# A four-part graph network on one core: three hops joined into one stream, and attention layers whose rows are prepared by finished node tiles

## The chip, the cores and the metric

The kernel runs on one core of one Trainium2 chip. The metric is device time in microseconds (us) of one execution; the time before is the median of three runs. Engines are named as the profile names them: PE (matrix products; PEld is its weight load), DVE (VectorE), ACT (ScalarE), POOL (GpSimd) and SP, whose queue issues most DMA transfers.

## The reference

A graph of 3125 nodes with 128 features each has 103125 edges (50000 in both directions and one loop per node), sorted by target. Four residual parts follow each other; every part takes the layer norm and relu of x and adds its result to x.

```python
h = jnp.maximum(_layernorm(x), 0.0)
x = x + hops(h)        # 3 hops:
    # left = agg[head] @ q_w;  right = tanh(rel * agg[tail] @ k_w)
    # w = softmax over the edges of a head of sum(left * right)
    # agg = segment_sum(w * rel * agg[tail], head) / max(count, 1)
    # agg = agg / max(norm(agg), 1e-12);  out = out + agg + h
h = jnp.maximum(_layernorm(x), 0.0)
x = x + gat(h)         # 3 layers, 4 heads of 32 features:
    # e = leaky_relu(alpha_s[src] + alpha_d[dst]);  softmax over the edges of a target
    # out = segment_sum(xs[src] * alpha, dst) + bias;  relu between layers
h = jnp.maximum(_layernorm(x), 0.0)
x = x + gcn(h)         # 2 graph convolutions with degree norms, then two dense layers
h = jnp.maximum(_layernorm(x), 0.0)
x = x + relation(h)    # one attention over the edges of a target with rel_emb, then tanh(. @ neigh_w)
```

## The kernel before, in words

**Tiling.** Nodes lie in T = 28 tiles of Q = 112 rows. First (to about 1010 us) the edges are counted and sorted into cells: one cell per pair of a target tile and a source tile, with up to 128 edges on the partitions. What does not fit its cell goes to OV = 3 overflow cells per column. A *column* is one node tile as the side that is summed over; it has NG = 8 *groups*, seven of K = 4 cells and one of the three overflow cells. Node tiles are also taken by *quads*, four at a time, seven quads in all (`quads()`).

**Gathering by matrix products.** Rows of nodes are held three times in bfloat16 (`parts`, split by `in_parts`, L738 to L741, two ACT copies and two DVE subtractions per quad), and one-hot matrices (`oh`, `own`) multiply them. Overflow rows come from a table in HBM with indirect DMAs of POOL's queue (`gather`, L703): `rows_d` for the hops, `gat_d` for the layers.

**Hops and the relation attention.** `attend` (L776) is called once per hop and once at the end. It is a software pipeline written out by hand: the list `order` holds pairs of a stage and a lag, and each step `i` runs the stage for group `i - lag`, so that the engines' queues hold instructions in just that order (`in_order`). The stages are: `s_load` (lag 0: one-hot loads, overflow gathers), `s_hot`, `s_rel`, `s_rows` (L828 on PE), `s_comb` (L836 DVE, times the relation), `s_turn` (L844 PE transposes, L846 ACT copy), `s_right` (L852 PE, L854 ACT Tanh), `s_score` (L860 PE, L862 DVE), `s_most` to `s_less` (maximum per node, L874 to L906 DVE), `s_exp` (L910 ACT Exp), and `s_sum` (lag 21, L918 PE), which at a column's end copies sum and denominator out of PSUM (L921, L922). 224 groups and 21 lags make 245 steps. In hop 0 further work rides along: relation rows, masks and degrees are made and kept in HBM for the later hops.

After each hop a tail for all tiles follows (L1074 to L1101): `over_in` once in hop 0 (its load is L684), r = 1 / denominator / count, agg times r, Square and reduce, Sqrt (L1090), agg times the reciprocal norm (L1094), the add to `xs` on POOL (L1096), `in_parts`, the store to `rows_d` (L1100) and `sides` (transposes L747, product with q_w L762, copy L763).

**The three layers.** The order here is a scheduler's: the program's order with priorities, under waits for data and for tile buffers of the pools `rows1` and `sums1`. `norm_relu` runs first. `layer_rows` (L1117 to L1148) per quad transposes h, multiplies by the layer's weights (L1135), copies (xw), splits into `parts` and stores `gat_d`; then it stores the alphas of all targets (L1145) and spreads them over 112 partitions as `arow` (L1148, four broadcasts). `layer_sums` (L1150) then goes through the columns. Each column is prepared: `c_load` (overflow gathers, `absent` load L1168), `c_rows` (one-hots L1179), in layer 0 also `c_hot` and seven `c_cells` (L1198 to L1236, counts and masks of the column, kept for the later layers), `c_most` (L1248, the greatest alpha of the present edges per head, two halves on DVE), `c_node`, `c_weights` (Exp at L1288). Its groups run `g_load` (eq), `g_rows` (L1305 PE), `g_weigh` (L1313 DVE, rows times the head's weight; L1316 ACT copy of the weights) and `g_sum` (L1325 PE), the last of a column followed by L1329 to L1336 (division, bias, relu). The add of the layers' result to `xs` comes after the third layer (L1372).

**GCN and end.** In the pool `work2` follow the degree norm n_src, the layer norm, the product with n_src (L1430), two `sum_rows`, the dense layers, and the layer norm for the relation attention; after that a tail (L1500 to L1513) divides, transposes, multiplies by nw, takes Tanh, adds to `xs`, and writes the output in two DMAs.

Of the kernel before, what the change touches and what calls it, by code (L numbers as in the profile page):

```python
# [16 lines left out]
P = 128  # L17
D = 128
# [424 lines left out]
def by_cells(ctx: ExitStack, tc: tile.TileContext, edges, x, E, edge_emb, q_w, k_w, Ws, Wd, att_s, att_d,  # L443
# [25 lines left out]
    rows_d = tc.dram_tile([NP, D], F32, name="rows_d")  # L469
    gat_d = tc.dram_tile([NP, D + H], F32, name="gat_d")  # L470
# [69 lines left out]
    kindD = node.tile([P, T, COL], I32, name="kindD")  # L540
    outO = node.tile([P, T, OV], I32, name="outO")
    inO = node.tile([P, T, OV], I32, name="inO")
    posO = node.tile([P, T, OV], I32, name="posO")
    movO = node.tile([P, T, OV, 4], F32, name="movO")
# [14 lines left out]
    def lay_out(rows, tab, pp, pname):  # L559
# [3 lines left out]
        nonlocal ownS, kindS  # L563
        edge = hop_.enter_context(tc.tile_pool(name="edge", bufs=1))
        ownS = edge.tile([P, T, COL], BF16, name="ownS")
        kindS = edge.tile([P, T, COL], I32, name="kindS")
        with tc.tile_pool(name="lay", bufs=1) as lp:
# [114 lines left out]
    def over_in():  # L682
        lay = work.tile([P, T, OV, 4], F32, name="layD", bufs=1)
        nc.sync.dma_start(lay, slots_o[:T * NO, :].rearrange("(s p k) f -> p s k f", p=P, k=OV))  # L684
        nc.vector.tensor_copy(overO[:, 0], lay[:, :, :, 0])
        nc.vector.tensor_sub(overO[:, 1], lay[:, :, :, 3], lay[:, :, :, 0])
        nc.vector.tensor_copy(kindD[:, :, T:], lay[:, :, :, 2])
        nc.vector.tensor_copy(inO, lay[:, :, :, 3])
        f = work.tile([P, T * OV], F32, name="fD", bufs=1)
        nc.vector.tensor_copy(f, lay[:, :, :, 1].rearrange("p s k -> p (s k)"))  # L690
        pt = pm.tile([P, K, P], F32, name="pm")
        nc.tensor.transpose(pt[:T * OV, 0, :], f, ident)
        rb = work.tile([T * OV, P], BF16, name="rbD", bufs=1)
        nc.scalar.copy(rb, pt[:T * OV, 0, :])
        nc.sync.dma_start(bass.AP(tensor=dst_own.tensor, offset=dst_own.offset + T * P,
                                  ap=[[COL * P, T], [P, OV], [1, P]]), rb)
# [68 lines left out]
    def row_tile(table, c, t0, n, p=Q, name="row", bufs=3):  # L765

        t = work.tile([p, HALF * P], BF16, name=name, bufs=bufs)
# [8 lines left out]
    def attend(oh_d, table, idx, side, den, sums, combine, rel_d, masks, rel_rows=None, right=None, aside=None,  # L776
               column_end=None):


        cols = {}  # L780
        groups = [(c, g) for c in range(T) for g in range(NG)]
        st = {}
        H1 = NG // 2
# [5 lines left out]
        def s_load(c, g):  # L789
# [6 lines left out]
            if g == 0:  # L796
                over_rows[c] = work.tile([P, OV, D], F32, name="orow", bufs=2)
                for k in range(OV):
                    gather(over_rows[c][:, k, :], table, idx[:, c, k:k + 1])
            if rel_rows:  # L800
                rel_rows[0](s, c, g)
            if aside:
                aside(c * NG + g)

        def s_hot(c, g):
# [4 lines left out]
            if rel_rows:  # L810
                rel_rows[1](st[c, g], c, g)

        def s_rel(c, g):
            s, m = st[c, g], width(g)
            if not rel_rows:
# [3 lines left out]
        def s_rows(c, g):  # L819
# [10 lines left out]
            if rel_rows:  # L830
                rel_rows[2](s, c, g)

        def s_comb(c, g):
            s, m = st[c, g], width(g)
            s["v"] = vs[(c * NG + g) % len(vs)]
            nc.vector.tensor_tensor(s["v"][:, :m, :D], s["rows"][:, :m, :], s["rel"][:, :m, :], combine)  # L836
            if rel_rows:
# [46 lines left out]
        def s_diag(c, g):  # L884
# [7 lines left out]
            if column_end:  # L892
# [19 lines left out]
        def s_sum(c, g):  # L912
# [7 lines left out]
            if g == NG - 1:  # L920
                nc.scalar.copy(sums[:, c, :], acc[:Q, :D])  # L921
                nc.scalar.copy(den[:, c:c + 1], acc[:Q, D:D + 1])  # L922
            del st[c, g]

        def mask(i):
# [4 lines left out]
        order = [(s_sum, 14 + w), (s_exp, 13 + w), (s_less, 12 + w), (s_spread_most, 11), (s_turn_most, 10), (s_most, 9),  # L930
                 (s_comb, 5), (s_score, 8), (s_diag, 10), (s_right, 7), (s_turn, 6), (mask(2), 7), (mask(1), 6),
                 (mask(0), 5), (s_rows, 4), (s_hot, 2), (s_rel, 3), (s_load, 0)]
        with in_order(tc):
            for i in range(len(groups) + order[0][1]):
                for f, d in order:
                    if 0 <= i - d < len(groups):
                        f(*groups[i - d])
# [6 lines left out]
    den = hops.tile([Q, T], F32, name="den")  # L944
# [3 lines left out]
    bank = work = ownS = kindS = None  # L948
# [24 lines left out]
    with tc.tile_pool(name="work0", bufs=3) as work:  # L973
# [95 lines left out]
        for hop in range(3):  # L1069
            attend(src_oh, rows_d, outO, side, den, agg, OP.mult, src_rel, (other_load, other_make, other_keep),  # L1070
                   None if hop else (rel_load, rel_hot, rel_make, rel_keep), kw,
                   rel_ahead if hop else over_by_target, None if hop else degree)
            kept_out()
            if hop == 0:  # L1074
                over_in()
                nc.vector.tensor_scalar_max(cnt, deg_src, 1.0)
                nc.vector.reciprocal(cnt, cnt)
            r = work.tile([Q, T], F32, name="r", bufs=1)
            nc.vector.tensor_scalar_max(r, den, 1e-30)
            nc.vector.reciprocal(r, r)  # L1080
            nc.vector.tensor_mul(r, r, cnt)
            nr = work.tile([Q, T], F32, name="nr", bufs=1)
            for n0, n1 in quads():
                m = n1 - n0
                nc.vector.tensor_mul(agg[:, n0:n1, :], agg[:, n0:n1, :],
                                     r[:, n0:n1].unsqueeze(2).to_broadcast([Q, m, D]))
                sq = work.tile([Q, K, D + H], F32, name="res", bufs=2)
                nc.scalar.activation(sq[:, :m, :D], agg[:, n0:n1, :], AF.Square)
                nc.vector.tensor_reduce(nr[:, n0:n1], sq[:, :m, :D], AX.X, OP.add)
            nc.scalar.activation(nr, nr, AF.Sqrt)  # L1090
            nc.vector.tensor_scalar_max(nr, nr, 1e-12)
            nc.vector.reciprocal(nr, nr)
            for n0, n1 in quads():
                nc.vector.tensor_mul(agg[:, n0:n1, :], agg[:, n0:n1, :],  # L1094
                                     nr[:, n0:n1].unsqueeze(2).to_broadcast([Q, n1 - n0, D]))
                nc.gpsimd.tensor_add(xs[:, n0:n1, :], xs[:, n0:n1, :], agg[:, n0:n1, :])  # L1096
                if hop < 2:
                    in_parts(agg, n0, n1)
            if hop < 2:
                nc.sync.dma_start(node_rows(rows_d), agg)  # L1100
                sides(agg, side, qw)  # L1101

    hop_.close()

    with tc.tile_pool(name="work1", bufs=1) as work1:
        h = big.tile([Q, T, D], F32, name="agg")
# [4 lines left out]
        brow = work1.tile([P, D], F32, name="brow")  # L1111
# [3 lines left out]
        def layer_rows(l):  # L1115

            af = work.tile([Q, H, T], F32, name="af", bufs=1)  # L1117
            wx = work.tile([P, W4 + H], F32, name="wx", bufs=1)
            for w_, a_, to in ((Ws, att_s, D), (Wd, att_d, W4)):
                w = work.tile([P, H, C], F32, name="wl", bufs=2)  # L1120
                nc.scalar.dma_start(w.rearrange("p h c -> p (h c)"), w_[l])
                a = work.tile([P, H, C], F32, name="al", bufs=2)
# [5 lines left out]
                nc.vector.tensor_reduce(wx[:, to:to + H], a, AX.X, OP.add)  # L1128
            nc.scalar.dma_start(brow, bass.AP(tensor=gat_b.tensor, offset=gat_b.offset + l * D, ap=[[0, P], [1, D]]))
            for n0, n1 in quads():  # L1130
                hT = transposed(h, n0, n1)
                xw = work.tile([Q, K, W4 + H], F32, name="xw", bufs=3)
                for n in range(n0, n1):
                    pw = pm.tile([P, 512], F32, name="pm")
                    nc.tensor.matmul(pw[:Q, :W4 + H], hT[:, n - n0, :], wx, start=True, stop=True)  # L1135
# [1082 lines left out]
```

## Time and profile before

| | us |
|---|---|
| median of 3 runs | 7420.47 (7419.32 to 7425.95) |
| the profiled execution | 7405.67, its span 7403.9 |
| counting, sorting, laying out | 0 to about 1030 |
| three hops and their tails | to about 3793 |
| three layers | to 6243 |
| GCN, dense layers | to about 6700 |
| relation attention, tail | to 7403.9 |
| column, hop 0 / hops 1 and 2 / relation | 34.2 / 29.5 / 22.9 |
| column, layer 0 / layers 1 and 2 | 34.9 / 21.3 |
| busy share: PE, DVE, ACT, POOL | 83%, 76%, 42%, 49% |

A column's time is the distance between the ends of two neighbouring columns, which is read from the instruction that closes each (L921 and L1331). Between the last column of a stage and the first of the next lies a *seam*. A row of a window reads: the window, its length, then for PE, PEld, DVE, ACT and POOL the busy us and the number of instructions, the granted clock of PE as a share, the busy share of the DMA engines, and GB/s. A group's row reads: line, engine, operation, output and inputs, shapes, count, busy us and mean ns, idle time before it with what ended it.

### The profile page before, as it was taken

How to read it: one execution, taken by the hardware profiler on the slowest of the kernel's cores; microseconds unless marked ns; L12 is line 12 of the kernel's file. 1: busy time of each engine (PE TensorE's matmuls, PEld its weight loads, DVE VectorE, ACT ScalarE, POOL GpSimd, SP SyncE). 2: the span in 40 equal slices, each digit the busy share in tenths (PEclk: the TensorE clock that was granted, in tenths of full speed). 3: DMA queues.
4: the chain of work that ended last, by engine and by line, in shares of the span. 5: the costliest groups of instructions: out<-in, count | busy, mean ns of one | idle time of the engine just before them, and what ended most of it. 6: DMA issues, size and time to landing. Idle time of an engine off the chain costs nothing. (4 is left out here: it accounts for less than half of the span.)

```text
span 7403.9 us, 157726 instructions
## 1 busy us (share of the span) xinstructions
PE 6157.7 (83%) x59400; PEld 5175.9 (70%) x59400; DVE 5642.0 (76%) x12038; ACT 3098.9 (42%) x8419; POOL 3645.8 (49%) x3360
## 2 busy tenths in 40 slices
PE   5877729999989998999957878857775776988998
PEld 3443328888878887888846777747775776767998
DVE  8887628888866666666658999969997998237887
ACT  3766514444444444444437777720001001114554
POOL 2777767665468885777833433314431332341110
PEclk9887759999999999999977898878886888999999
DMA  2100025554467775777747888757766775556665
GB/s 64 25 19 17 12 54 156 151 148 145 135 175 208 204 208 146 213 208 203 205 116 231 242 246 255 239 163 211 205 192 175 207 204 163 144 151 183 213 213 155
DMA packets 686935, 1222.52 MB, mean 165 GB/s; under 512 B 129398, under 2 KB 450056, under 8 KB 684820
## 3 DMA queue, kind: packets, MB, share of 16 engines
q1 hardware_dynamic: 567060, 996.40, 45.5%
q0 software_dynamic: 109120, 208.86, 11.3%
q8 instruction: 473, 7.75, 0.5%
q10 hardware_dynamic: 9984, 7.07, 0.3%
q14 instruction: 298, 2.44, 0.1%
HBM read 915.61 MB, written 296.27 MB: 164 GB/s over the span
## 5 line engine op out<-in xcount | busy, mean ns | idle before, releaser
L1248 DVE CUSTOM_DVE_ANT_0 junk<-arow,absent 112x1568 bf16<-112x1568 f32 x672 | 1203.6, 1791 | 58.6 <-DMA absent<-absent_d 54.7
L1325 PE MATMUL pa<-v,eq 128*112 128x132 f32 x5208 | 831.1, 308 | 333.9 <-ACT v L1316 236.9
L703 POOL DMA_INDIRECT ahead<-in_L_gnn_rel_emb_dram,kindD x868 | 961.1, 1107 | 265.7 <-issue 254.7
L862 DVE SCALAR_TENSOR_TENSOR z<-other,pm 128x448 f32<-128x448 bf16 (+1 forms) x896 | 541.8, 605 | 617.2 <-PE pm L860 429.0
L1325 PEld LDWEIGHTS pa<-v,eq 128*112 128x112 f32 x5208 | 709.9, 198 | 372.1 <-ACT v L1316 247.8
L918 PE MATMUL pa<-v,z 128*112 128x129 f32 x6944 | 949.1, 279 | 4.6 <-ACT z L910 4.6
L854 ACT ACTIVATE right<-pm 128x512 f32<-128x512 f32 (+1 forms) x672 | 392.7, 584 | 1297.5 <-PE pm L852 1295.5
L703 POOL DMA_INDIRECT orow<-gat_d,inO x252 | 465.2, 1846 | 927.4 <-DVE ndp L1264 600.4
L918 PEld LDWEIGHTS pa<-v,z 128*112 128x112 f32 x6944 | 817.4, 177 | 20.3 <-ACT z L910 5.8
L373 POOL DMA_INDIRECT slots<-pay,pos x610 | 669.7, 1098 | 266.0 <-issue 182.2
L860 PE MATMUL pm<-side,right 128*128 128x112 f32 x5208 | 686.3, 274 | 4.3 <-DVE z L862 3.3
L844 PEld LDWEIGHTS pm<-ident,v 128*128 128x128 f32 x3472 | 431.3, 143 | 363.0 <-issue 274.6
L852 PE MATMUL pm<-vT,kw 128*128 128x512 f32 (+1 forms) x1344 | 684.2, 591 | 0.8 <-DVE z L862 0.8
L828 PE MATMUL pg<-parts,oh 112*128 112x128 bf16 x9408 | 663.9, 220 | 22.4 <-DMA oh<-src_oh 15.3
L1305 PE MATMUL pg<-parts,oh 112*128 112x128 bf16 x7056 | 557.7, 233 | 106.3 <-DMA oh<-oh_d 35.0
L860 PEld LDWEIGHTS pm<-side,right 128*128 128x128 f32 x5208 | 634.9, 192 | 6.1 <-issue 3.4
L846 ACT COPY vT<-pm 128x512 f32<-128x512 f32 (+1 forms) x896 | 511.3, 571 | 293.7 <-PE pm L844 221.7
L828 PEld LDWEIGHTS <-oh 112*128 112x128 bf16 x9408 | 600.2, 98 | 33.3 <-issue 24.2
L836 DVE TENSOR_TENSOR v<-pg,rel 128x512 f32<-128x512 f32 x700 | 479.7, 685 | 170.5 <-PE pg L828 111.6
L703 POOL DMA_INDIRECT orow<-rows_d,inO x252 | 241.1, 957 | 745.0 <-DVE v L836 484.1
L1305 PEld LDWEIGHTS <-oh 112*128 112x128 bf16 x7056 | 502.4, 106 | 111.4 <-issue 97.2
L844 PE MATMUL pm<-ident,v 128*128 128x128 f32 x3472 | 528.6, 274 | 22.5 <-DVE v L836 22.3
(372 smaller groups left out, 12645.9 us busy)
## 6 DMA issues: line engine op xcount, KB each, us to landing
eq<-eq_d SPq DMA_DIRECT2D x784, 224.0 KB
rel<-src_rel SPq DMA_DIRECT2D x392, 256.0 KB
dst_rel<-ahead POOLq DMA_DIRECT2D x196, 256.0 KB
rel<-dst_rel SPq DMA_DIRECT2D x196, 256.0 KB
other<-other_d SPq DMA_DIRECT2D x392, 112.0 KB
eq_d<-eqf SPq DMA_DIRECT2D x196, 224.0 KB
absent<-absent_d SPq DMA_DIRECT2D x56, 686.0 KB
ct<-count_d SPq DMA_DIRECT2D x56, 686.0 KB
```

What stands on the lines that cost most here:

```text
L373: st = nc.gpsimd.indirect_dma_start(out=slots, out_offset=bass.IndirectOffsetOnAxis(ap=pos[:m, k:k + 1], axis=0), in_=pay[:m, k0 + k, :], ...
L703: return nc.gpsimd.indirect_dma_start(out=to, out_offset=None, in_=table, in_offset=bass.IndirectOffsetOnAxis(ap=index, axis=0))
L828: nc.tensor.matmul(pg[:, k, :], h["oh"][:, (e0 + k) * P:(e0 + k + 1) * P], parts[:, g * K + k, i, :D], start=(i == 0), stop=(i == 2))
L844: nc.tensor.transpose(pT[:, k, :], s["v"][:, k, :D], ident)
L846: nc.scalar.copy(s["vT"][:, :m, :], pT[:, :m, :])
L852: nc.tensor.matmul(pK[:, :m, :], right, s["vT"][:, :m, :], start=True, stop=True)
L860: nc.tensor.matmul(pS[:, k, :], s["vT"][:, k, :], side[:, c, :], start=True, stop=True)
L862: nc.vector.scalar_tensor_tensor(s["z"], s.pop("other")[:, :m, :], MASK, pS[:, :m, :], op0=OP.mult, op1=OP.add)
L918: nc.tensor.matmul(acc[:Q, :D + 1], s["z"][:, k, :], s["v"][:, k, :], start=(g == 0 and k == 0), stop=(g == NG - 1 and k == m - 1))
L1248: nc.vector.tensor_tensor_reduce(junk, arow[:, hd, half], c["absent"][:, half], 1.0, -3e38, OP.subtract, OP.max, accum_out=c["am"][:, j, h ...
L1305: nc.tensor.matmul(pg[:, k, :], c["oh", g * K // HALF][:, (e0 + k) * P:(e0 + k + 1) * P], parts[:, g * K + k, i, :D], start=(i == 0), stop ...
L1325: nc.tensor.matmul(acc, s["eq"][:, k, :], s["v"][:, k, :], start=(g == 0 and k == 0), stop=(g == NG - 1 and k == m - 1))
```

## The change

**Hops as one stream.** `attend` takes a list of tables (`rows_d`, a new `rows_e`, `rows_d`) and runs all hops in one sequence: a hop starts 240 steps after the one before, 733 steps in all. What was the tail becomes stages behind `s_sum`, for a column each (`weight`, `mean`) or for a quad each (`root`, `unit`, `turned`, `by_q`, `normed`, `relu`), one step apart. The layer norm before the layers is done by them in hop 2. The splitting of quads 0 to 5 follows in the last steps of a hop. The add to `xs` goes from POOL to DVE, and `mean` scales on ACT and sums the squares with its accumulator. `over_in` is cut into four pieces spread over the last 40 steps of hop 0.

**Layers.** Layer 0's first column is prepared before the layer's rows. Alphas are made per finished quad within the layer before (`alpha_rows`), and spread per quad in its last steps; between layers the last quad's alphas and the rows of all quads are left. In the last layer `layer_out` adds to `xs`, norms and multiplies by n_src per quad. `c_most` goes by halves; the overflow gathers go from `c_load` to a preparing step. eq has 4 buffers instead of 5 and orow and xw 2 instead of 3. In layers 1 and 2, `g_weigh` of the even groups is done on ACT, in 16 activations of 128x32 each.

**End.** The relation attention's tail runs in the stream by quads, the output with one DMA per quad.

```diff
-        order = [(s_sum, 14 + w), (s_exp, 13 + w), (s_less, 12 + w), (s_spread_most, 11), (s_turn_most, 10), (s_most, 9),
+        order = [(ended(f), 15 + w + k) for k, f in reversed(list(enumerate(finish)))] + [
+                 (s_sum, 14 + w), (s_exp, 13 + w), (s_less, 12 + w), (s_spread_most, 11), (s_turn_most, 10), (s_most, 9),
                  (s_comb, 5), (s_score, 8), (s_diag, 10), (s_right, 7), (s_turn, 6), (mask(2), 7), (mask(1), 6),
-                 (mask(0), 5), (s_rows, 4), (s_hot, 2), (s_rel, 3), (s_load, 0)]
+                 (mask(0), 5), (s_rows, 4), (s_over(0, 0), 10), (s_over(1, 1), 4), (s_hot, 2), (s_rel, 3), (s_load, 0),
+                 (s_over(2, T), 0)]
+        A = T * NG + AFTER - 1
         with in_order(tc):
-            for i in range(len(groups) + order[0][1]):
+            for i in range(len(tables) * A - AFTER + 1 + order[0][1]):
                 for f, d in order:
-                    if 0 <= i - d < len(groups):
-                        f(*groups[i - d])
+                    hop, u = divmod(i - d, A)
+                    if 0 <= hop < len(tables) and u < T * NG:
+                        f(*divmod(u, NG))
+                hop, u = divmod(i, A)
+                if extra:
+                    extra(hop, u)
...
+        def extra(hop, u):
+            if hop == 0 and u >= T * NG - 40 and u % 4 == 0:
+                next(over, None)
+            if hop == 0 and u == T * NG + 8:
+                kept_out()
+            q = u - T * NG + 1
+            if hop < 2 and 0 <= q < T // K - 1:
+                in_parts(agg, q * K, q * K + K)
+
+        def weight(c, acc):
...
+            nc.vector.tensor_scalar_max(r, acc[:, D:D + 1], 1e-30)
             nc.vector.reciprocal(r, r)
+            nc.vector.tensor_mul(r, r, cnt[:, c:c + 1])
+
+        def mean(c, acc):
+            nc.scalar.activation(agg[:, c, :], acc[:, :D], AF.Copy, scale=over_one.pop(c))
+            sq = work.tile([Q, K, D + H], F32, name="res", bufs=2)[:, 0, :D]
+            nc.scalar.activation(sq, agg[:, c, :], AF.Square, accum_out=nr[:, c:c + 1])
+
+        def root(n0, n1):
+            nc.scalar.activation(nr[:, n0:n1], nr[:, n0:n1], AF.Sqrt)
+
+        def unit(n0, n1):
+            nc.vector.tensor_scalar_max(nr[:, n0:n1], nr[:, n0:n1], 1e-12)
+            nc.vector.reciprocal(nr[:, n0:n1], nr[:, n0:n1])
+            nc.vector.tensor_mul(agg[:, n0:n1, :], agg[:, n0:n1, :],
+                                 nr[:, n0:n1].unsqueeze(2).to_broadcast([Q, K, D]))
+            nc.vector.tensor_add(xs[:, n0:n1, :], xs[:, n0:n1, :], agg[:, n0:n1, :])
+
+        def turned(n0, n1):
+            if hop < 2:
+                nc.sync.dma_start(node_rows(tables[hop + 1])[:, n0:n1, :], agg[:, n0:n1, :])
+                nexts[n0] = transposed(agg, n0, n1)
+            else:
...
+        def by_q(n0, n1):
+            if hop < 2:
+                pw = pm.tile([P, K, P], F32, name="pm")
+                nc.tensor.matmul(pw[:, :, :Q], qw, nexts.pop(n0), start=True, stop=True)
+                nc.scalar.copy(side[:, n0:n1, :], pw[:, :, :Q])
+                if n1 == T:
                     in_parts(agg, n0, n1)
+            else:
+                nc.scalar.activation(nexts[n0][:, :, 1], nexts[n0][:, :, 1], AF.Sqrt, bias=eps[:Q])
...
+        def alpha_rows(wx, n0, n1):
+            hT = transposed(h, n0, n1)
+            m = (n1 - n0) * Q
+            pa = pm.tile([P, 512], F32, name="pm")
+            nc.tensor.matmul(pa[:H, :m], wx[:, D:W4], hT[:, :n1 - n0, :], start=True, stop=True)
...
+            nc.sync.dma_start(alpha_d[:, n0 * Q:n0 * Q + m], at)
...
+        def layer_out(n0, n1):
+            m = n1 - n0
+            nc.gpsimd.tensor_add(xs[:, n0:n1, :], xs[:, n0:n1, :], h[:, n0:n1, :])
...
+            nc.scalar.activation(rs[:, :m], mv[:, :m, 1], AF.Sqrt, bias=eps[:Q])
...
-                s["eq"] = work.tile([P, K, Q], F32, name="eq", bufs=5)
+                s["eq"] = work.tile([P, K, Q], F32, name="eq", bufs=4)
...
-                nc.vector.tensor_mul(s["v"][:, :m, :D].rearrange("p k (h c) -> p k h c", h=H),
-                                     s["rows"][:, :m, :].rearrange("p k (h c) -> p k h c", h=H),
-                                     w.unsqueeze(3).to_broadcast([P, m, H, C]))
+                if not first and g % 2 == 0:
+                    for k in range(m):
+                        for hd in range(H):
+                            o = slice(hd * C, (hd + 1) * C)
+                            nc.scalar.activation(s["v"][:, k, o], s["rows"][:, k, o], AF.Copy, scale=w[:, k, hd:hd + 1])
+                else:
+                    nc.vector.tensor_mul(s["v"][:, :m, :D].rearrange("p k (h c) -> p k h c", h=H),
+                                         s["rows"][:, :m, :].rearrange("p k (h c) -> p k h c", h=H),
+                                         w.unsqueeze(3).to_broadcast([P, m, H, C]))
                 nc.scalar.copy(s["v"][:, :m, D:], w)
...
+            steps = layer_sums(0, brow, pool, next_rows)
+            for _ in range(NG + 6):
+                next(steps)
+            for n0, n1 in quads():
+                hT = alpha_rows(wx, n0, n1)
+                alpha_spread(n0, n1)
+                layer_rows(wx, n0, n1, hT)
+            for l in range(L):
...
+                for left in steps:
+                    while made and left > -5:
+                        alpha_spread(*made.pop(0))
+                while made:
+                    alpha_spread(*made.pop(0))
...
+                if l < L - 1:
+                    for n0, n1 in quads():
+                        layer_rows(wx, n0, n1)
+                    steps = layer_sums(l + 1, nrow, pool, next_rows if l + 1 < L - 1 else layer_out)
```

## The prediction

> **What bounds the kernel now.** I read the page's 40 slices first, then busy time by window over each stage and over the stretch between two stages (a seam), then the chain of work within the seams, then the groups and waits of a steady stretch. Column ends come from the last copy of a column's sum (hops: L921; layers: the division L1331), read one by one in the timeline.
>
> In the slices PE is at nine tenths or more through the hops but drops where one stage ends; DVE is full in the layers:
>
> ```profile
> PE   5877729999989998999957878857775776988998
> DVE  8887628888866666666658999969997998237887
> PEclk9887759999999999999977898878886888999999
> ```
>
> The windows (PE, PEld, DVE, ACT, POOL busy us, granted clock, DMA share) give the bound of each stretch: steady hop, seam between two hops, hops to layers, layer 0, layer to layer, steady layer 1, layers to GCN, the end.
>
> ```profile
> 2033.00:2084.00 51.00, 28.32 (x146) 19.88 (x147) 35.68 (x61) 26.87 (x51) 17.55 (x14) 0.67 0.20 54
> 2300.00:2880.00 580.00, 580.00 (x5140) 499.97 (x5138) 391.32 (x709) 251.89 (x530) 455.44 (x451) 1.00 0.71 206
> 3780.00:3978.00 198.00, 93.19 (x784) 76.89 (x783) 130.58 (x316) 101.57 (x228) 52.42 (x41) 0.59 0.52 158
> 4000.00:4849.00 849.00, 682.16 (x8299) 600.11 (x8298) 800.14 (x1475) 651.31 (x1681) 318.14 (x291) 0.90 0.80 244
> 4888.00:5003.00 115.00, 40.72 (x373) 37.00 (x373) 72.67 (x160) 14.51 (x36) 12.37 (x13) 0.58 0.60 167
> 5003.00:5560.00 557.00, 424.28 (x5423) 407.81 (x5422) 541.32 (x1133) 51.14 (x265) 214.50 (x128) 0.89 0.74 201
> 6243.00:6288.00 45.00, 16.45 (x68) 11.29 (x69) 31.48 (x123) 15.50 (x27) 11.26 (x13) 0.66 0.48 129
> 7372.00:7404.00 32.00, 11.67 (x93) 9.82 (x91) 9.65 (x16) 7.58 (x16) 0.00 (x0) 0.81 0.20 53
> ```
>
> A steady hop is PE's alone (580 of 580 us at clock 1.00); layers 1 and 2 are DVE's (541 of 557) with ACT nearly idle (51); in the seams no engine is full and the clock falls to 0.56-0.67. What sets the seams before layers 0 and 1, in the chain of work:
>
> ```profile
> 3855.71 26.58 DMA own<-dst_own
> ...
> 4925.26 24.70 DMA absent<-absent_d
> ```
>
> Both are loads queued on SP behind the broadcasts of arow (L1148); DVE's prep work waits for them. Steady layer 1, 26 columns, and two of its waits:
>
> ```profile
> L1248 DVE CUSTOM_DVE_ANT_0 junk<-arow,absent 112x1568 bf16<-112x1568 f32 x198 | 353.4, 1785 | 0.0
> L1325 PE MATMUL pa<-v,eq 128*112 128x132 f32 x1572 | 254.7, 311 | 132.2 <-ACT v L1316 109.2 <-issue 21.3 <-DMA eq<-eq_d 0.8
> L1313 DVE TENSOR_TENSOR v<-pg,w 128x512 f32<-128x512 f32 x177 | 118.3, 680 | 10.6 <-PE pg L1305 9.4 <-PE pm L1274 0.9
> ```
>
> ```profile
> ACT w L1288 <- DVE em L1287: 247.6, 52, 8.4
> ```
>
> **The change, part by part.** The profiled execution took 7405.67 us (span 7403.9); the median is 7420.47, 14.8 above, and I add that at the end.
>
> *Two seams between hops.* From the last column's end to the next hop's first is 2040.48 to 2149.80 = 109.3 us. The next hop's first steady rows (L828) start near 2085, so 64.5 us is the fill of the pipeline and 44.8 is serial tail: r and agg*r (7 x 0.68), Square and reduce (7 x 0.63 + 0.68), Sqrt, in_parts (2.9 us of DVE per quad), transposes and sides. The tail now rides in the stream by quads; only the last quad's is left, and 16 steps of the next hop's loads and rows are already under way. Still to pay: 28 transposes and 7 matmuls of L762 on the full PE (about 6 us a hop), and the last quad's chain of eight stages, -2 to 8 beyond the fill. That leaves 44.8 - 6 - 2 = about 37 per seam: **-75** for two (50 to 90).
>
> *Hop 0's gap.* One column takes 40.4 us instead of 34.2: SP waits from 1741.8 for slots_o with the layD load (L684), and later loads queue behind it. The load now comes near the end of the hop: **-6**.
>
> *New work in the hop stream.* ACT runs Sqrt once per quad (28 times with hop 2's second one) between Tanh and Exp. The timeline around L1090 prices a switch:
>
> ```profile
> 2049.24 0.63 ACT L1088 ACTIVATE res<-agg 112x512 f32<-112x512 f32 x1 [0.57 <-DVE agg L1085]
> 2049.88 1.28 ACT L1090 ACT_TABLE_LOAD   x1
> 2051.18 0.23 ACT L1090 ACTIVATE nr<-nr 112x28 f32<-112x28 f32 x1
> ```
>
> There and back is 2 x 1.28 + 0.23 = 2.8 us. In a steady step (3.69 us) ACT works 1.75 and L846's result is needed 1.5 to 1.7 us after it is ready, so PE, which is the bound, stalls about 2.8 - 1.7 = 1.1 at each of the 21 in hops 1 and 2 and less in hop 0 (step 4.28): **+20** (0 if the cover is wider, 28 x 2.8 = 78 if there is none). Unit and the xs add (from POOL L1096 to DVE, 0.68 each) lie under PE: DVE is at 391 of 580. The Trainium skill ("ScalarE: Activation LUTs", What ACT_TABLE_LOAD costs) puts a switch at 1.28 us of load plus 1.38 of drain and says to batch calls by table set, which speaks against a Sqrt in every quad. By it each Sqrt would block 5.5 us and this term would be about +105. The rows above show Sqrt 0.02 us after the load and the load 0.01 us after Square, so I go by the row.
>
> *Hops to layer 0.* Before, 197.05 us from 3780.57 to 3977.62: tail and norm to 3818, layer_rows to 3851, then 26.6 us for own, hot and seven c_cells of 4.1 us, c_most, weights, sums. Now column 0's oh and own load ahead of arow, and its cells run before the rows. What stays in a row: last quad 12, first loads 5, cells 29, layer_rows on DVE 26, c_most 8 x 1.79 = 14, weights 8, first sums 37: 131. **-66** (45 to 85; if the pool's release makes the loads late the low end).
>
> *Layer to layer.* Before 114.6 (4888.23 to 5002.85) and 116.9. Alphas and arow of quads 0 to 5 move into the previous layer, absent loads ahead of the last alpha. Left: last alpha 5, layer_rows and c_most on DVE 26 + 14, weights 8, sums 21: 74. **-80** for two (50 to 100). Moved onto layers 0 and 1 are 7 x 4 transposes and 7 DMAs each, in PE's idle 24%.
>
> *Layer 2 to GCN.* The norm and n_src product move into the stream by quad (about 2 us of DVE per quad there, which is full); rows_d's store (8.05 us) stays: **-10** (5 to 15).
>
> *The end.* 31.2 us from the last column to the end; the last quad's division, transposes, Tanh, add and a DMA of one quad take about 13: **-18** (10 to 25).
>
> *Half the weighing of layers 1 and 2 to ACT.* DVE loses four L1313 per column (4 x 0.6 = 2.4 of 21.3): 18.9 by DVE alone. Each even group becomes 16 activations of 128x32 with a scale operand, which the trace lacks. Back to back, L1219 (128x112, scale operand) starts every 0.279 us and L394 (128x128) every 0.292: 0.0008 per element, so 0.21 for 32 elements, 3.4 per group. Ends: 0.094, as L1316's small copies start, gives 1.5 per group; L1219's full duration, 0.383, gives 6.1. I take 0.21, the row with the same operand. The sum of a group (L1325, 0.94 for four) waits for it, and in PE's order the rows of the next even group (L1305, 0.67) stand behind that sum, so a pair of groups takes 3.4 + 0.94 + 0.67 = 5.0 and a column 20.0, plus 0.2 as Exp (L1288), which waits for DVE, stands in ACT's order among the activations: 20.2, a gain of 1.1 x 56 = **-62** (18.9 gives -134; no gain gives 0; 6.1 per group gives 31 us, +540). The Trainium skill (same page, Rules for kernel authors) gives mul to VectorE, not ScalarE. By it the sum would be 0 here instead of -62; against it stands that DVE is full and ACT idle.
>
> *Layer 0 and buffers.* eq goes from 5 buffers to 4, orow and xw from 3 to 2. A load of eq then starts four groups ahead of its sum, 10.6 us; PE's row shows 0.8 us waited for eq in 26 columns. Layer 0 (34.9 a column, DVE 94%) may go 1 us either way: **0** (-28 to +28).
>
> Sum: -75 - 6 + 20 - 66 - 80 - 10 - 18 - 62 = -297. 7405.7 - 297 = 7108.7, plus 14.8: **7123 us**, 4.0% below 7420.47.
>
> **Rivals.**
> - *Offload eaten.* If Exp stuck behind activations, or the chain through PE, holds layer 1 columns at 21.3, the seams alone count: 7123 + 62 = 7185. For it: ACT already waits 247.6 us for DVE's em (longest 8.4), and now the weighing stands behind that wait. Against: ACT has 506 of 557 us free.
> - *Offload whole.* Columns at DVE's 18.9: 7123 - 72 = 7051. For it: ACT's 13.6 us a column fits; against: PE's order.
> - *Seams half.* The last quad's chain and the loads' releases stay serial and every Sqrt stalls PE by its whole 2.8: +58 for the Sqrts, the seam terms at their low ends +25 +21 +30: 7257.
> - *Slower.* The activations cost their full 0.383 as in L1219, with no overlap, since each writes a slice of the same tile: 31 us a column, 7185 + 540 = 7725. It decides from 235 / 56 = 4.2 us a column over 21.3, that is 0.30 us per activation. Against: neighbours with the same operand in the trace start 0.279 apart even at 112 elements.
>
> **How the numbers follow.** Forecast 0.50, offload eaten 0.27, whole 0.10, seams half 0.09, slower 0.04. The range reaches from 7040 (offload whole) to 7250 (near seams half); outside it lie the slower case, half of the seams-half case and the low ends of every seam together, about 0.15. A measurement of this kernel can tell about 0.2% from no change. Faster 0.95, same 0.01, slower 0.04: only the last rival ends above 7420.
>
> **What would show it.** Of the changed kernel: hop 0's last column to hop 1's first some 72 us instead of 109, with the clock near 1.00; 28 table-load pairs with PE idle up to 1.1 behind each; no wait over 10 us for own or absent; layers 1 and 2 with L1313's successor at half its count, columns of 20.2, ACT near 16 us a column. The prediction fails if PE's sums in layers 1 and 2 wait for the activations beyond 3.4 us a group, if eq or oh end waits in layer 0, or if ACT's table loads slow the hops by more than 3 us a quad.

## The result and the profile after

The changed kernel takes 7343.14 us (median of four runs, 7341.27 to 7351.63) against 7419.90 (four runs beside them): a ratio of 0.9898, 95% interval 0.9886 to 0.9910. It is 77 us faster; 297 were forecast, and 7343 lies above the range's end of 7250. The profiled execution took 7342.68, its span 7340.9.

The same windows of the changed kernel (a seam between hops, steady hop 1, hops to layer 0, layer 0, layer to layer, layer 1, the end; columns as before):

```profile
2045.00:2095.00 50.00, 47.53 (x412) 38.58 (x410) 35.08 (x62) 22.56 (x43) 33.05 (x34) 1.00 0.75 219
2300.00:2860.00 560.00, 559.36 (x4925) 480.72 (x4925) 389.30 (x754) 268.44 (x556) 446.09 (x436) 1.00 0.71 204
3716.00:3866.00 150.00, 89.75 (x732) 67.77 (x732) 95.89 (x210) 94.54 (x213) 36.46 (x30) 0.68 0.70 200
3900.00:4850.00 950.00, 702.63 (x8013) 613.99 (x8010) 767.59 (x1408) 633.16 (x1627) 317.88 (x282) 0.84 0.69 211
4939.00:5014.00 75.00, 41.69 (x369) 35.77 (x369) 66.98 (x138) 26.24 (x98) 12.98 (x9) 0.64 0.63 173
5030.00:5540.00 510.00, 407.80 (x5041) 370.00 (x5038) 463.62 (x980) 321.97 (x1817) 207.59 (x125) 0.90 0.80 213
7328.00:7341.00 13.00, 2.69 (x21) 2.10 (x19) 1.02 (x3) 1.50 (x3) 0.00 (x0) 0.69 0.10 24
```

The seam between hops is PE's now (47.5 of 50 us, clock 1.00; before, 28 of 51 at 0.67). But in layer 0 no engine is full any more: DVE was at 800 of 849 and is at 768 of 950.

Where the time went, from the start of each column's last sum matmul (L918 and L1325 before, L935 and L1442 after) to that of the next stage's, in us:

| stretch | before | after | gain | forecast |
|---|---|---|---|---|
| start to hop 0's first column | 1156.1 | 1141.7 | 14.4 | 0 |
| hop 0, first to last column | 884.1 | 898.5 | -14.4 | 6, less stalls |
| two seams between hops | 219.2 | 145.8 | 73.4 | 75 with the PE work of the stream in it |
| hops 1 and 2 | 1521.0 | 1530.2 | -9.2 | -20 for all hops |
| hop 2 to layer 0's first column | 194.7 | 149.4 | 45.3 | 66 |
| layer 0, first to last column | 912.5 | 1073.2 | **-160.7** | 0 (-28 to 28) |
| two seams between layers | 228.0 | 148.5 | 79.5 | 80 |
| layer 1 / layer 2 | 562.3 / 564.5 | 562.7 / 552.2 | -0.4 / 12.3 | 62 for both |
| layer 2 to the relation's first column | 536.8 | 526.3 | 10.5 | 10 |
| relation attention | 593.2 | 599.6 | -6.4 | 0 |
| last column to the end | 31.5 | 12.5 | 19.0 | 18 |

The gains sum to 63, as the spans do (7403.9 - 7340.9). The relation's columns that close a quad take 1.2 us more (24.1 in place of 22.9), PE's new work there, which the sum had left out. Most seams came near their forecast, the one from the hops to layer 0 fell 21 short; layer 0 lost 161, and layers 1 and 2 together gained 12 in place of 62. In layer 0 the columns alternate, some 48 and 34 us, where before they ran between 29 and 44 in threes. The waits of the stretch 4000 to 4849 of before, and of 3900 to 4850 of after (engine, line, what it waited for: us in total, times, longest):

```profile
ACT hot L1201 <- PE pm L1198: 68.0, 41, 5.8
PE pm L1198 <- DVE own L1187: 12.6, 18, 2.1
```

```profile
ACT hot L1311 <- PE pm L1308: 205.7, 50, 13.3
PE pm L1308 <- DVE own L1297: 63.2, 11, 7.2
```

In 11 columns of some 23, PE stands up to 7.2 us at the transposes of the one-hot `own`, and ACT behind it. DVE's timeline at one of these places:

```profile
4129.62 1.78 DVE L1359 CUSTOM_DVE_ANT_0 junk<-arow,absent 112x1568 bf16<-112x1568 f32 x1
4131.33 0.75 DVE L1297 TENSOR_SCALAR own<-own,iota_p 112x2048 bf16<-112x2048 bf16 x1
4132.00 1.78 DVE L1359 CUSTOM_DVE_ANT_0 junk<-arow,absent 112x1568 bf16<-112x1568 f32 x1
...
4136.53 0.62 DVE L1297 TENSOR_SCALAR oh<-oh,iota_p 112x1536 bf16<-112x1536 bf16 x1 [2.74 <-DMA oh<-dst_oh]
4137.06 1.78 DVE L1359 CUSTOM_DVE_ANT_0 junk<-arow,absent 112x1568 bf16<-112x1568 f32 x1
4138.78 0.71 DVE L1297 TENSOR_SCALAR own<-own,iota_p 112x1920 bf16<-112x1920 bf16 x1
```

The one-hots of the coming column stand in DVE's queue between the reductions of `c_most` (1.78 each), and one of them waits for its load, which SP issued at 4131.74, right behind two eq loads that held its queue for 3.46 us. That they stand between reductions is not new by itself: in the kernel before they do too (its timeline from 4435 to 4446 has own, reduction, own, two reductions, oh, which waits 0.92). What is new is the order. In DVE's timeline of layer 0 the sequence of one-hots and reductions repeats about every three columns in the kernel before and every two in the changed one. Between the last oh of one column and the first own of the next stands at most one reduction before, and four or six in turn after. Four edits could be behind it: four eq buffers, the new order of `c_most`, the late overflow gathers, the alphas per quad.

### The profile page after: what moved, and what is told of

It is laid out like the page before. It is cut to its first block, busy times and chain, and to the rows that moved or that the text cites. A ratio compares the mean times of both kernels' runs of the same rounds, so it can differ in the third digit from the quotient of the medians.

```text
span 7340.9 us, 161470 instructions
## 1 busy us (share of the span) xinstructions
PE 6244.2 (85%) x59495; PEld 5200.1 (71%) x59495; DVE 5521.5 (75%) x12113; ACT 3838.1 (52%) x12186; POOL 3688.5 (50%) x3346
## 4 chain that ended last, share of the span: by engine, by line
PE 59%; DVE 10%; ACT 8%; DMA 4%; issue 3%; POOL 1%; ACTq 0%; SPq 0%; DVEq 0%; POOLq 0%
PE pa L935 11%; PE pm L877 10%; PE pm L869 7%; PE pg L845 7%; PE pa L1442 6%; DVE junk L1359 5%; PE pm L861 5%; ACT v L1428 3%; PE pg L1416 3%; PE pa L1550 2%; PE pm L1047 1%; DMA oh<-dst_oh 1%; ACT hot L1311 1%; PE pm L1340 1%; DMA eq<-eq_d 1%
## 5 line engine op out<-in xcount | busy, mean ns | idle before, releaser
L1359 DVE CUSTOM_DVE_ANT_0 junk<-arow,absent 112x1568 bf16<-112x1568 f32 x672 | 1231.9, 1833 | 10.8 <-DMA arow<-alpha_d 9.6
L708 POOL DMA_INDIRECT ahead<-in_L_gnn_rel_emb_dram,kindD x868 | 991.7, 1143 | 266.6 <-issue 256.6
L1442 PE MATMUL pa<-v,eq 128*112 128x132 f32 x5208 | 900.8, 316 | 122.5 <-ACT v L1433 34.3
L935 PE MATMUL pa<-v,z 128*112 128x129 f32 x6944 | 951.0, 279 | 12.1 <-ACT z L927 12.0
L1442 PEld LDWEIGHTS pa<-v,eq 128*112 128x112 f32 x5208 | 733.4, 201 | 187.1 <-ACT v L1428 69.8
L935 PEld LDWEIGHTS pa<-v,z 128*112 128x112 f32 x6944 | 820.2, 177 | 34.1 <-ACT z L927 16.3
L1428 ACT ACTIVATE v<-pg,w 128x32 f32<-128x32 f32 x3584 | 670.2, 343 | 203.6 <-PE pg L1416 193.3
L708 POOL DMA_INDIRECT orow<-gat_d,inO x252 | 375.3, 1489 | 798.1 <-DVE v L1430 310.5
L1416 PE MATMUL pg<-parts,oh 112*128 112x128 bf16 x7056 | 582.1, 232 | 170.2 <-DVE v L1430 127.8
L845 PE MATMUL pg<-parts,oh 112*128 112x128 bf16 x9408 | 659.1, 220 | 11.4 <-DVE oh L826 7.8
L863 ACT COPY vT<-pm 128x512 f32<-128x512 f32 (+1 forms) x896 | 510.8, 570 | 272.0 <-PE pm L861 198.9
L845 PEld LDWEIGHTS <-oh 112*128 112x128 bf16 x9408 | 595.9, 98 | 21.7 <-issue 12.5
L1326 POOL TENSOR_TENSOR spread<-lo,hi 128x448 bf16<-128x448 bf16 x196 | 253.3, 1296 | 703.4 <-PE pm L1340 403.9
```

The lines of the kernel that those rows point to most:

```text
L708: return nc.gpsimd.indirect_dma_start(out=to, out_offset=None, in_=table, in_offset=bass.IndirectOffsetOnAxis(ap=index, axis=0))
L845: nc.tensor.matmul(pg[:, k, :], h["oh"][:, (e0 + k) * P:(e0 + k + 1) * P], parts[:, g * K + k, i, :D], start=(i == 0), stop=(i == 2))
L935: nc.tensor.matmul(acc[:Q, :D + 1], s["z"][:, k, :], s["v"][:, k, :], start=(g == 0 and k == 0), stop=(g == NG - 1 and k == m - 1))
L1359: nc.vector.tensor_tensor_reduce(junk, arow[:, hd, half], c["absent"][:, half], 1.0, -3e38, OP.subtract, OP.max, accum_out=c["am"][:, j, h ...
L1416: nc.tensor.matmul(pg[:, k, :], c["oh", g * K // HALF][:, (e0 + k) * P:(e0 + k + 1) * P], parts[:, g * K + k, i, :D], start=(i == 0), stop ...
L1428: nc.scalar.activation(s["v"][:, k, o], s["rows"][:, k, o], AF.Copy, scale=w[:, k, hd:hd + 1])
```

## The experiments

In the runs of the experiments, on other chips or at other times than the two profiles above, the sorting and the hops are slower in every kernel (the kernel before takes 8470 to 8810 us there, 979 to 1084 for each of hops 1 and 2 instead of 760), while the layers agree with the first profile (before, unedited: 902.2, 559.5, 565.4). So the layers are compared by stretches and not by the whole time; the last three runs are on the hops themselves.

**Five eq buffers again, in the changed kernel.**

```diff
-                s["eq"] = work.tile([P, K, Q], F32, name="eq", bufs=4)
+                s["eq"] = work.tile([P, K, Q], F32, name="eq", bufs=5)
```

> The changed kernel with five buffers for eq in the layers again, as before. Theory A (one buffer fewer makes SP wait for a later sum, and the one-hot loads queued behind that eq load come late, so that DVE and PE stand): layer 0, 41 us a column in the changed kernel, falls to 34 to 36, and the whole time by 120 to 160 us, to about 7180 to 7220. Theory B (the new order of the column's preparation and the two orow buffers are the cause): layer 0 stays within 1 us of 41 a column, and the whole time above 7310. Theory C (the alphas per quad, for which PE waits): as B.

Layer 0 took 1073.6 us. Theory A falls: with the rest of the changed kernel as it is, the buffer is not what layer 0 waits for.

**Four eq buffers in the kernel before** (the reverse edit).

> The kernel before with four buffers for eq in the layers and nothing else. Theory A: layer 0 grows from 34 to 39 to 41 us a column, the whole time to 7520 to 7600. Theory B or C: layer 0 within 1 us of 34 a column, the whole time within 30 us of the kernel before.

Layer 0 took 942.9, 30 to 41 more than 912.5 and 902.2. The buffer alone costs 1.1 to 1.5 us a column, a little over the 1 us bounded in the prediction, and not 161 us; layers 1 and 2 (562.4, 567.0) do not feel it.

**The work of a finished quad one column later.**

```diff
-                    if d % K == K - 1 or d == T - 1:
-                        done(d // K * K, d + 1)
+                    if d % K == 0 and d > 0:
+                        done(d - K, d)
+                    if d == T - 1:
+                        done(d // K * K, d + 1)
```

> The changed kernel with the work of a finished quad (alphas, or in the last layer its norm) issued one column later, so that PE no longer stands at its transposes until POOL has added the bias and taken the relu. Theory C: the columns that close a quad, 24 to 26 us against 18 to 21 in layer 1, lose their extra 5 to 6 us; layer 1 shortens by 25 to 40 us from 563, layer 0 by 10 to 60, the whole time by 50 to 100. Theory A or B: layer 0 stays within 15 us; layer 1 shortens by at most 10.

Layer 0 stayed (1089.2, 16 more), layer 1 fell to 539.5, by 23 from the first profile (562.7) and by 20 from a later one (559.7). Theory C fails in layer 0 and holds in part in layer 1. Layer 2, where the edit delays its norm, took 577.3 (552.2 and 575.2 in two executions of the changed kernel), which tells nothing.

**All weighing on DVE again** (`if False:` in place of the test for even groups).

> The changed kernel with all weighing on DVE again. If the offload is worth what its columns between quads show (18 to 20 us against 21.3) and the alphas took it back, layer 1 grows from 563 to 600 or more and the whole time by 50 to 80 us. If the offload gains nothing, layers 1 and 2 stay within 10 us each.

Layers 1 and 2 took 588.8 and 581.3: layer 1 26 to 29 more than 562.7 and 559.7, but short of the 600 expected, layer 2 6 to 29 more than 575.2 and 552.2, the two executions of the changed kernel, which differ by 23 themselves. In layer 1 the offload is worth having, and the layer around it got dearer by about as much; in layer 2 its worth is not shown by this run.

**The changed kernel again**, on the chip of the three runs after it.

> The changed kernel again, unedited, as the measure for the three beside it on the same chip. The stages of the layers are expected as in its first profile: 1073 us from the end of layer 0's first column to its last, 563 in layer 1, 552 in layer 2, each within 15 us.

1076.0, 559.7 and 575.2 in the layers. As a whole it stands at 1.0167 of the kernel before there (1.0109 to 1.0226), 132 us more by the medians: on these chips the change makes the kernel slower. Layer 0 alone lost 164 to 174 (1076.0 against 912.5 and 902.2); the hops lose too, of which below.

**Overflow gathers at the head of the preparation, three orow buffers.**

```diff
                 c = cols[d] = {}
+                if d > 1 or not first:
+                    c_over(d)
...
-                rows = cols[d]["rows"] = work.tile([P, OV, W4], F32, name="orow", bufs=2)
+                rows = cols[d]["rows"] = work.tile([P, OV, W4], F32, name="orow", bufs=3)
```

> The changed kernel with the overflow gathers of the layers back at the head of a column's preparation (but for layer 0's first two columns) and three orow buffers. Theory B1 (gathers late, on two buffers, in POOL's queue between the spreads): layer 0 falls from 1073 us by 80 to 160. Theory B2 (the greatest alpha by halves): within 20 us of 1073. Theory D (no single edit: the prepared first column and the alphas moved the columns' phase): within 40 us of 1073.

Layer 0 took 1072.9 us: theory B1 falls.

**The greatest alpha by heads.**

```diff
-                j = i // 2
-                for hd in range(i % 2 * 2, i % 2 * 2 + 2):
+                hd = i
+                for j in range(2):
```

> The changed kernel with the greatest alpha taken head by head again. Theory B2: layer 0 falls from 1073 us by 80 to 160, since an absent tile is again read as a whole. Theory B1: within 20 us of 1073. Theory D: within 40.

Layer 0 fell to 957.6, by 118. Its waits from 5200 to 5960 (760 us of layer 0) stand against 186.8 and 63.4 us in 900 us (5200 to 6100) of the unedited changed kernel beside it:

```profile
ACT hot L1311 <- PE pm L1308: 36.7, 29, 2.5
PEld L1308 <- DVE own L1297: 20.8, 15, 2.3
```

**Both edits together.**

> Both of these edits undone together, with eq still on four buffers. Theory B1 or B2: layer 0 at 915 to 950 us. Theory D: above 1030, and the cause lies in the first column before the rows or in the work per quad.

955.7 us, no better than the heads alone (957.6), and just over the 950 expected. What is left above 912.5 and 902.2 is 43 to 54. Four eq buffers cost 30 to 41 in the kernel before, but they are not most of it here: the last run of the layers below has the heads and five buffers in layer 0 and takes 949.5, 8 less than the heads alone. So some 40 us of layer 0 stay without a shown cause; the alphas per quad were not tried there without the halves.

**The halves alone, in the kernel before.**

```diff
-                for j in range(2):
+                j = i // 2
+                for hd in range(i % 2 * 2, i % 2 * 2 + 2):
```

> The kernel before with nothing but the greatest alpha taken by halves of the absent tile, as in the changed kernel. If the halves are the cause by themselves, layer 0 grows from 912 us by 80 to 160; if they only hurt together with the other edits of the changed kernel, it grows by less than 40. Layers 1 and 2 (562 and 564): within 20 us.

Layer 0 took 1080.3 us, 168 to 178 more than 912.5 and 902.2 and a little over the 80 to 160 expected, with columns of 47 and 36 in turn as in the changed kernel and with four or six reductions in turn between the last oh and the next own; layers 1 and 2 stayed at 564.0 and 564.1. Its waits from 5100 to 6000 are those of the changed kernel too:

```profile
ACT hot L1201 <- PE pm L1198: 211.9, 53, 12.4
PE pm L1198 <- DVE own L1187: 66.2, 11, 6.5
```

Windows of layer 0, first with the halves, then in the unedited kernel before on another of these chips:

```profile
5100.00:6000.00 900.00, 643.82 (x7264) 575.78 (x7263) 710.63 (x1313) 578.32 (x1478) 305.16 (x256) 0.83 0.68 205
```

```profile
5400.00:6100.00 700.00, 561.18 (x6907) 492.25 (x6905) 651.72 (x1231) 539.04 (x1392) 267.61 (x245) 0.91 0.81 248
```

One edit of two lines, which adds no instruction, takes DVE from 93% (651.72 of 700) to 79% (710.63 of 900) of the stage. By itself it makes a loss as large as layer 0's 161; in the changed kernel, where other edits stand beside it, undoing it brings 118 back, so the losses don't add.

**The offload alone, in the kernel before.**

> The kernel before with nothing but the even groups' weighing of layers 1 and 2 on ACT. By the price found in the changed kernel (26 to 29 us a layer), layers 1 and 2 fall from 562 and 564 to 530 to 540. By the prediction's term (62 for both) the same; if PE's order eats it, 555 or more.

Layer 1 took 519.9, 40 to 42 less and below the 530 to 540 expected, with columns of 18.0 to 21.5; layer 2 took 559.3, only 5 to 6 less. There the columns settle into pairs of about 24 and 18 to 20, and ACT waits 81.8 us for Exp's input (L1287) in place of 50.8 in layer 1; why layer 2 falls into this and layer 1 does not stays open. The whole stands at 0.9949 of before (0.9923 to 0.9975).

**The edits put together:** halves in layers 1 and 2 only, five eq buffers, layer 1's alphas late.

```diff
-                j = i // 2
-                for hd in range(i % 2 * 2, i % 2 * 2 + 2):
+                for j, hd in ([(0, i), (1, i)] if first else [(i // 2, i % 2 * 2), (i // 2, i % 2 * 2 + 1)]):
```

> The changed kernel with the greatest alpha by heads in layer 0 and by halves in layers 1 and 2, five buffers for eq, and the alphas of layer 1 issued one column late. Expected: layer 0 at 920 to 960 us, layer 1 at 535 to 550, layer 2 as in the changed kernel (552 to 577), the whole 120 to 180 us below the changed kernel of the same chip.

Layer 0 949.5, layer 1 538.2, layer 2 568.3: 127, 22 and 7 us less than the changed kernel's 1076.0, 559.7 and 575.2. The whole is at 0.9979 of the kernel before (0.9958 to 1.0000), where the changed kernel, on another chip, was at 1.0167. Measured against the kernel before on its own chip, it beats the changed kernel; that it beats the one before isn't shown, and it had no run with quick hops. By its stages (127 + 22 + 7) it would be about 150 us below 7343 there, an estimate.

**The hops without POOL's gathers.** The runs above hold comparisons on one chip, since their edits leave the hops alone. Beside e2, with the old hops at 982.1 and 984.9, the three runs of the changed kernel (e1, e3, e4) take 1156 to 1164 in hop 1 and 1045 to 1049 in hop 2. Beside g1 and g2 (998 to 1005, 979 to 983) g3 takes 1150.0 and 1031.7. So where the hops are slow, the change makes hop 1 dearer by 145 to 182 us and hop 2 by 49 to 64. In hop 1 of the changed kernel there (2700 to 3700) ACT and PE stand for nothing that the profile names:

```profile
ACT right L871 <- remote: 305.7, 38, 13.3
PE pm L877 <- issue: 100.5, 40, 4.2
```

The three runs: the kernel before unedited, and both kernels with zeros in place of the relation rows that POOL gathers in hops 1 and 2.

```diff
-                for k in range(width(g)):
-                    gather(t[:, k, :], rel_emb, kindD[:, c, g * K + k:g * K + k + 1])
+                nc.gpsimd.memset(t, 0.0)
```

> The kernel before, unedited, for its stages on the chip of these runs: hops 1 and 2 at 980 to 1005 us each, layers as in its first profile (912, 562, 564) within 15.

The layers came within the 15 us expected; the hops, at 1084.0 and 1080.3, lie above the 980 to 1005 expected, though this run has the same chip number as e2, with 982.1 and 984.9.

> The changed kernel without POOL's gathers of relation rows in hops 1 and 2 (a fill with zeros stands in their place, so the last attention works on wrong relation rows). If these gathers starve PE and ACT, hops 1 and 2 fall to 760 to 800 us each and the seams to 73. If the stalls come from the stream's new work (table loads, small instructions), hop 1 stays above 1050.

> The kernel before without the same gathers (zeros in their place). If the gathers are the cause, hops 1 and 2 fall to 760 to 790 each and the changed kernel's hops and seams together are again 60 us or more shorter than these. If not, they stay at 980 or more.

| us | hop 1 | hop 2 | seams |
|---|---|---|---|
| before, unedited | 1084.0 | 1080.3 | 186.8, 186.7 |
| before, no gathers | 760.5 | 760.5 | 109.8, 109.9 |
| changed, unedited | 1158.7 | 1079.8 | 132.5, 132.3 |
| changed, no gathers | 770.2 | 760.1 | 73.5, 72.9 |

Without the gathers every stretch of this table has the value of the first profiles to within a microsecond, and the changed kernel's hops and seams are 64 us shorter than those of the kernel before. Hop 0, whose gathers were left in, stays slow (1092.0 and 1053.6). PE never stands (the second window; the first is the unedited changed kernel):

```profile
2700.00:3700.00 1000.00, 803.17 (x5741) 650.01 (x5740) 455.16 (x879) 313.59 (x640) 465.69 (x498) 0.81 0.45 133
```

```profile
2700.00:3300.00 600.00, 600.00 (x5293) 515.77 (x5290) 415.78 (x808) 284.73 (x591) 145.54 (x226) 1.00 0.57 170
```

POOL's indirect gathers, with the traffic that they bring, are what slows hops 1 and 2 there, in both kernels. A gather itself takes no longer (1.02 to 1.04 us on average in 500 us of these hops, 1.12 to 1.14 in the first profiles). Why they do so in these runs and not in the first profiles, whether by the chip or by the time (982 and 1084 us under one chip number), and by which path they hold up PE and ACT, stays open. The unedited pair of the table ran on two chips, so its difference in hop 1 (1158.7 against 1084.0) is no measure of the change; the pairs on one chip above are.

## Why the prediction was wrong

*Seams between layers, the end, layer 2 to GCN:* right, to a microsecond each (79.5 of 80, 19.0 of 18, 10.5 of 10). *Seams between hops:* 73.4 of 75, in part by luck. The 75 had 12 us of new PE work taken off, which falls for the most part into the hops and not into the seams; without it the forecast for these two stretches was some 86. Hops and their seams together gained about 50, where the sum had 61 (75 + 6 - 20).

*New work in the hop stream:* the size was near (30 us lost on new work in hops 0 and 1, against 20 for the Sqrts and 12 in the seams), its working was not. A Sqrt per quad was to stall PE by 1.1 us. Hop 2 has 14 of them and took 760.1 us, 0.4 less than before; the timeline there shows the whole switch,

```profile
3055.34 1.28 ACT L1126 ACT_TABLE_LOAD   x1
3056.63 0.20 ACT L1126 ACTIVATE nr<-nr 112x4 f32<-112x4 f32 x1
3056.86 1.28 ACT L927 ACT_TABLE_LOAD   x1
```

and PE is busy for all of 2960 to 3700:

```profile
2960.00:3700.00 740.00, 740.00 (x6535) 637.30 (x6534) 530.02 (x1079) 363.91 (x745) 581.66 (x553) 1.00 0.69 199
```

So the 2.8 us, which the durations confirm, are covered whole, and the Sqrt term is 0 in this hop. The page "ScalarE: Activation LUTs" of the Trainium skill (What ACT_TABLE_LOAD costs) would have 1.38 us of drain with each switch; here the load starts as L863 ends at 3055.33, and the next activation 0.01 us after the load. Hop 1's 9.6 us are of the size of the 28 transposes and 7 products on PE (3.9 and 6.8 us busy from 2190 to 2990), forecast at 6; hop 2, without them, lost nothing. In hop 0 the 6.2 us of the late load came, against 20.6 lost in the columns that end a quad and at the hop's end. The 14.4 us ahead of hop 0's first column I hadn't seen: in before DVE waits 23.5 us at once for gathers of relation rows, with the overflow gathers of two columns ahead of them in POOL's queue, and the change puts these later. That the order of POOL's queue is the reason is argued.

*Hops to layer 0:* 149 against 131 forecast. The chain of waits has what the sum left out, the way of the alphas through HBM, 14.0 us where 18 were missed:

```profile
3783.82 7.85 DMA alpha_d<-aT
3791.69 6.15 DMA arow<-alpha_d
```

*Layer 0:* this is the step that failed. The prediction costed the buffers and gave 0 (-28 to +28) to the stage; the new order inside `c_most` it priced at nothing and named no work that hides it. The buffers cost a little more than was bounded (30 to 41 us in the kernel before, alone; 0 and 8 in the two runs of the changed kernel). The order costs 168 us alone in the kernel before, and 118 of the 161 come back when it alone is undone; the other 43 stay open. How it hits is argued from the waits: DVE is 94% busy in the kernel before, and in its timeline which reductions stand ahead of the next column's one-hots decides when PE and ACT can go on (PE's wait for `own` grows from 12.6 to 63.2 us, and to 66.2 with the halves alone). The prediction's own sign of failure came with it: DVE's wait for the load of oh in layer 0 grew from 13.5 us to 43.3 in the same windows. That halves change DVE's order is seen in its timeline; why the scheduler's order comes out so that every second column is hit was not tried.

*Half the weighing to ACT:* mechanism and price were right in layer 1, the net wasn't. In layer 1 of after (5030 to 5540):

```profile
L1428 ACT ACTIVATE v<-pg,w 128x32 f32<-128x32 f32 x1559 | 291.6, 340 | 90.2 <-PE pg L1416 86.3 <-PE pm L1388 3.1
L1430 DVE TENSOR_TENSOR v<-pg,w 128x512 f32<-128x512 f32 x73 | 49.9, 683 | 33.9 <-PE pg L1416 25.1 <-ACT v L1433 4.3 <-ACT v L1428 2.3
```

An activation lasts 0.34 us, but neighbours overlap: the chain has sixteen in 2.96 us, 0.185 each, against 0.21 taken. In the kernel before the offload alone gives 40 to 42 us in layer 1 (31 forecast), in layer 2 only 5 to 6 (31 forecast), 45 to 48 of the 62. The term that failed in layer 1 is the one put at nothing, the alphas "in PE's idle 24%". They don't fall into idle time: PE's queue reaches the transposes (L752) while POOL still takes the bias and relu of the quad's last column, and everything behind them waits.

```profile
PE pm L752 <- POOL agg L1453: 29.2, 6, 5.6
```

The columns that close a quad take 24 to 26 us instead of 18 to 22; issued a column later the alphas give back 20 to 23 us of layer 1. In layer 2 the norm per quad stands in their place; what it costs there was not shown.

*Rivals.* "Offload eaten" described layers 1 and 2 rightly in its price, not in its cause. None of the rivals held layer 0's order, which is why 7343 fell outside: without layer 0's 161 us the kernel would stand at 7182, beside that rival's 7185.

## What to carry to other kernels

Where an engine is almost full, as DVE was here at 94%, an edit that only reorders its instructions is a term of the sum like any other: price it from what it can push behind a 1.8 us instruction, or test it alone. Work placed "in the idle time" of an engine whose queue holds it in a fixed order, as PE's did here with 29.2 us of waits at the transposes, costs the wait at its own input, so place it after its producer is done, not when its data could be ready. And attribute a large change by stage: of some 230 us missed, layer 0 has 161, of which 118 come back with two lines, layers 1 and 2 have 50, and the seam into layer 0 has 21.

## What was not expected of the hardware

- In the runs of the experiments POOL's indirect gathers take a hop from 760 us to as much as 1170, by waits without a named cause (ACT 305.7 us in 1000); without them 770.2, 760.1 and 760.5 return. The first profiles show the same gathers and hops of 760 to 770.
- Two table loads and a Sqrt, 2.8 us of ACT in a step of 3.7, cost PE nothing in hop 2, where they come twice a quad (PE busy for 740 of 740 us from 2960 to 3700).
- Taking the same eight reductions of a column in another order costs 168 us over 28 columns (912.5 to 1080.3).
